# Order of VectorE's work on a stretch of attention scores: four mask additions in a row, the running maxima behind them

## The chip, the cores and the metric

The kernel runs on one core of a Trainium2 chip, in fp32 throughout. The metric is the device time of one execution in microseconds (us), as the median of several runs. Five engines work side by side, each through its own queue in order: TensorE (PE: matmuls, with weight loads shown as PEld), VectorE (DVE), ScalarE (ACT), GpSimd (POOL) and SyncE (SP, which here issues the transfers). They wait for one another through semaphores.

## The reference, cut to what matters

One block of a network over 32 batch elements of 64 tokens of width 256, with a context of 1601 keys for each element:

```python
x = x + cross_attention(layernorm(x), ctx, ctx, mask, ...)   # 16 heads of 16, 1601 keys
x = x + span_attention(layernorm(x), ...)                    # 64 keys, scores from a distance
x = x + ffn(layernorm(x), ...)                               # shared part and 8 experts
```

In the cross attention the scores are `q @ k / 4`; where the mask is false a score is set to a very low value; the softmax runs over the 1601 keys; and its weights form a sum over the values. Queries, keys and values have biases. The kernel adds a mask term (0 or -1e30) to the scores, subtracts the maximum over the keys, takes the exponential, and divides by the sum at the end.

## The kernel before, in words

**Tiling.** The unit of the cross attention is a *half*: one batch element `b` and eight of its sixteen heads (`c` is 0 or 1), so 64 halves, numbered `n`. The keys are cut into 13 blocks of 124, which stand on the partitions, and the blocks into four groups of 4, 3, 3 and 3 (`GROUPS`). One half's work on one group is a *stretch*, with `g` from 0 to 3. In a stretch, `scores` makes the scores of four pairs of heads in four banks of PSUM; VectorE adds the mask term and writes the result into SBUF (`prob`, L487, the *add*), four adds to a stretch.

**Pipeline.** Iteration `n` of the main loop (L678 on) makes the scores of half `n + 1` in its four stretches and meanwhile finishes half `n`. The maximum over the keys is formed in two steps. First VectorE keeps a running maximum over blocks in `mrun`, a bank of PSUM (`maximum`, L508): block 0 is copied there by ScalarE (`first_maxima`, L500), blocks 1 to 12 follow one by one, and the twelfth goes into `mx` in SBUF. Each reads what the one before it wrote. Then TensorE turns `mx` (`pm`, L515), VectorE reduces it along rows (`mc`, L522), TensorE spreads the result (`pb`, L530), and ScalarE copies it out (`mb`, L534). GpSimd subtracts `mb` from the four pairs of half `n` (L539, one pair in each stretch), ScalarE takes exponentials (L544), and TensorE multiplies by the values (`values`, L554): for half `n - 1`, heads 0 to 3 at the start of iteration `n`, heads 4 to 7 behind `pb` in the first stretch.

**Around it.** In every stretch TensorE also projects the keys of a following element (`pk`, L443), and in most its values (`pv`, L459). What follows the cross attention of two elements (normalisation, span attention) is cut into small steps which `run` hands out at the end of a stretch (`span_steps`, `query_steps`, `finish_steps`); many are short VectorE operations (L179 to L346, L627 to L635). The pattern of steps repeats every four iterations, since one tile of 128 tokens holds two elements of two halves each. Iterations are called R0, R1, R2 and R3 here, after `n` modulo 4.

**What sets the order.** The order on TensorE, VectorE, ScalarE and GpSimd is that of the code (`manual_schedule`). The tiles of `mm_bank` share six banks of PSUM (`ps_x`); which bank a tile gets is decided when the program is built. A matmul waits until the bank's last reader is done: VectorE for scores, ScalarE for `pk` and `pv`. Scores of the next stretch therefore wait for adds of the stretch before. The matmuls of a stretch run over blocks outside and over the four banks inside, so the first block already touches all four.

**Maxima before.** In stretches 1, 2 and 3 three blocks each have their maximum taken in `scores`, one behind each of the first three adds; these blocks come from the group before. The last three blocks follow at the end of the iteration. In stretch 0 there are only adds, with the reduction L522 behind the second.

Of the kernel before, what the change touches and what calls it, by code (L numbers as in the profile page):

```python
# [30 lines left out]
NKC = 13  # L31
KPAD = CHUNK * NKC
GROUPS = [(0, 4), (4, 3), (7, 3), (10, 3)]
BETWEEN = [(), (1, 2, 3), (4, 5, 6), (7, 8, 9), (10, 11, 12)]
LN_EPS = 1e-5
MASKED = -1e30
BIG = 3e38
# [37 lines left out]
def perceiver_kernel(ctx: ExitStack, tc: tile.TileContext, a: dict[str, bass.AP], out: bass.AP):  # L75
# [16 lines left out]
    def mm_bank(name: str):  # L92
        return ps_mm.tile([P, 512], F32, tag="mm", name=name)
# [277 lines left out]
    def pair_of(n: int, j: int):  # L371
        return prob[:CHUNK, place(n, j // 2), j % 2]

    def block_of(n: int, k: int):

        first, last = place(n, 0), place(n, 1)
        return prob[:CHUNK, first : last + 1 : last - first, :, k, :]
# [23 lines left out]
    def query_steps(t: int):  # L401
        spread = spread_of(xs[t], f"q{t}")
        yield 1
        xn = normalised(xs[t], spread, f"q{t}")
        yield 1
        ps = transposed(xn, f"q{t}")
        xnT = work.tile([P, 2, P], F32, tag="xnT", name=f"xnT_{t}")
        nc.vector.tensor_copy(xnT, ps)
        yield 1
        pq = mm_bank(f"pq_{t}")  # L410
        for c in range(2):
            for i in range(2):
                nc.tensor.matmul(
                    pq[:, c * P : (c + 1) * P], lhsT=wqT[:, i, c * P : (c + 1) * P],
                    rhs=xnT[:, i, :], start=(i == 0), stop=(i == 1),
                )

        q = work.tile([P, 2, 2, 2, S], F32, tag="qbd", name=f"qbd_{t}")
        for c in range(2):
            for e in range(2):  # L420
                nc.scalar.activation(
                    q[:, c, :, e, :], pq[:, c * P : (c + 1) * P].rearrange("p (b q) -> p b q", b=2),
                    AF.Identity, bias=bq4[:, c, e : e + 1], scale=own4[:, e : e + 1],
                )
        qbd[t] = q
        yield 1

        nc.gpsimd.tensor_tensor(xs[t], xs[t], bo_row, ALU.add)

    def load_context(b: int):  # L430
        for g in range(len(GROUPS)):
            load_piece(b, g)
        if b % 2 == 0 and b // 2 + 1 < NTILE:
            t = b // 2 + 1
            load_x(t)

    def project_keys(b: int, c: int, g: int):

        c0, n = GROUPS[g]
        k0, kn = c0 * CHUNK, min(n * CHUNK, KEYS - c0 * CHUNK)  # L440
        ps = mm_bank(f"pk_{b}_{c}_{g}")
        for i in range(2):
            nc.tensor.matmul(  # L443
                ps[:, :kn], lhsT=wkT[:, i, c * P : (c + 1) * P], rhs=cts[b][g][:, i, :kn],
                start=(i == 0), stop=(i == 1),
            )
        nc.scalar.activation(  # L447
            kTs[c][:, k0 : k0 + kn], ps[:, :kn], AF.Identity, bias=cols[:, B_K + c : B_K + c + 1]
        )
# [17 lines left out]
            ps[:kn, : n * D].rearrange("p (n h d) -> p n h d", n=n, d=DK),  # L467
        )

    def scores(n: int, g: int, between=(), then=None):  # L470

        b, c = halves[n]
        c0, nb = GROUPS[g]
        pss = [mm_bank(f"psc_{b}_{c}_{g}_{j}") for j in range(4)]
        for k in range(nb):
            for j, ps in enumerate(pss):
                at = (c0 + k) * CHUNK
                nc.tensor.matmul(  # L478
                    ps[:CHUNK, k * P : (k + 1) * P],
                    lhsT=kTs[c][32 * j : 32 * j + 32, at : at + CHUNK],  # L480
                    rhs=qbd[b // 2][32 * j : 32 * j + 32, c, b % 2, :, :],
                    start=True, stop=True, tile_position=(32 * j, 0),
                )
        between = deque(between)
        held = then() if then else None
        for j, ps in enumerate(pss):
            nc.vector.tensor_tensor(  # L487
                pair_of(n, j)[:, c0 : c0 + nb, :].rearrange("p k (e q) -> p k e q", e=2),
                ps[:CHUNK, : nb * P].rearrange("p (k e q) -> p k e q", k=nb, e=2),
                madd[:CHUNK, c0 : c0 + nb, None, :].to_broadcast([CHUNK, nb, 2, S]), ALU.add,  # L490
            )
            if between:
                maximum(n, between.popleft())
            if j == 1 and held is not None:
                maxima_of_rows(*held)

    mxs: dict[int, bass.AP] = {}

    def first_maxima(n: int):
        nc.scalar.copy(mrun[:CHUNK].rearrange("p (r i) q -> p r i q", r=2), block_of(n, 0))  # L500

    def maximum(n: int, k: int):

        dst = mrun
        if k == NKC - 1:
            dst = mxs[n] = work.tile([P, 4, P], F32, tag="mx", bufs=1, name="mx")
        dst, run = (m[:CHUNK].rearrange("p (r i) q -> p r i q", r=2) for m in (dst, mrun))
        nc.vector.tensor_tensor(dst, block_of(n, k), run, ALU.max)  # L508

    def turned_maxima(n: int):  # L510

        m = mxs.pop(n)
        ps = mm_bank("pm")
        for j in range(4):
            nc.tensor.transpose(  # L515
                ps[:, j * CHUNK : (j + 1) * CHUNK], m[:CHUNK, j, :], ident[:CHUNK, :CHUNK]
            )
        return ps, work.tile([P, 4], F32, tag="mc", name="mc")

    def maxima_of_rows(ps, col):  # L520

        nc.vector.tensor_reduce(  # L522
            col, ps[:, : 4 * CHUNK].rearrange("p (j k) -> p j k", j=4), AX.X, ALU.max
        )
# [18 lines left out]
    def exponentials(n: int, j: int):  # L543
        nc.scalar.activation(pair_of(n, j), pair_of(n, j), AF.Exp)  # L544

    def values(n: int, r: int):

        b, c = halves[n]
        v = vs[b % 2]
        for k in range(NKC):  # L550
            kn = min(CHUNK, KEYS - k * CHUNK)
            for j in range(4):
                h = 4 * r + j
                nc.tensor.matmul(  # L554
                    pvs[32 * j : 32 * j + DK + 1, c, :, r, :],
                    lhsT=v[:kn, k, 8 * c + h, :],
                    rhs=pair_of(n, h // 2)[:kn, k, (h % 2) * S : (h % 2) * S + S],
                    start=(k == 0), stop=(k == NKC - 1), tile_position=(0, 32 * j),
                )
# [95 lines left out]
        project_keys(0, 0, g)  # L655
        next(queries)
    for g in range(len(GROUPS)):
        scores(0, g, BETWEEN[g])
        if g == 0:
            first_maxima(0)  # L660
        project_keys(0, 1, g)
    for k in BETWEEN[-1]:
        maximum(0, k)

    pb = mm_bank("pbv")
# [12 lines left out]
    for n, (b, c) in enumerate(halves[:-1]):  # L678
        if c == 0 and b + 1 < B:
            load_context(b + 1)  # L680
        if c and b % 2 == 0 and b // 2 + 1 < NTILE:
            agenda[4 * n + 1].append(query_steps(b // 2 + 1))

        def project(f, *args):
            if b + 1 < B:
                f(b + 1, *args)

        if n:
            values(n - 1, 0)
            exponentials(n - 1, 3)  # L690
        for g in range(len(GROUPS)):
            if g == 0:
                turned = []

                def turn():
                    turned.extend(turned_maxima(n))
                    return turned

                scores(n + 1, g, BETWEEN[g], turn)
                project(project_keys, c, 0)  # L700
                m = maxima_along_rows(turned[1])
                if n:
                    values(n - 1, 1)
                    if c == 0:
                        agenda[4 * n + 1].append(finish_steps(b - 1, 4 * n + 1))
            else:
                scores(n + 1, g, BETWEEN[g])
                project(project_keys, c, g)
                if g == 1:
                    project(project_values, 3 * c)  # L710
                elif g == 2 and c:
                    project(project_values, 4)
                elif g == 3:
                    for u in range(5 if c else 1, 7 if c else 3):
                        project(project_values, u)
            less_maxima(n, g, m, nc.gpsimd)
            run(4 * n + g)
            for u in extra.get(4 * n + g, ()):
                linear_factor(u)
            if g == 0:  # L720
                first_maxima(n + 1)
            else:
                exponentials(n, g - 1)
        for k in BETWEEN[-1]:
            maximum(n + 1, k)


# [174 lines left out]
```

## Time and profile before

| | us |
|---|---|
| median of 3 runs | 1612.97 (1610.87 to 1616.4) |
| profiled execution, its own time | 1611.86 |
| its span, first to last instruction | 1609.8 |
| TensorE busy (matmuls) | 1548.2 |
| VectorE busy | 1260.5 |
| GpSimd busy | 1118.8 |
| ScalarE busy | 900.4 |
| adds (L487), 1024 | 582.2 |
| running maxima (L508), 704 and 64 | 483.4 and 43.9 |

"Busy" is time in which an instruction of the engine runs. Ends of matmuls are modelled, so a busy TensorE can still be waiting in part. "Idle before" a group is the engine's idle time just ahead of it, with what ended it. A timeline lists instructions in order of time with start, duration and number. A view by windows gives, for each stretch of time, the busy time of each engine, the clock granted to TensorE (1.00 is full) and the share of the DMA engines. The mean granted clock of the execution is 0.993.

### The profile page before, as it was taken

Reading aid. Unit: us, or ns where it says so; the run is one execution under the profiler, and the core shown is the slowest. Engines: PE = TensorE matmul, PEld = TensorE weight load, DVE = VectorE, ACT = ScalarE, POOL = GpSimd, SP = SyncE. Lnnn points to the kernel's source line nnn. Section 1 sums busy time; section 2 is a strip of 40 time slices with the busy share of each in tenths; the row PEclk is TensorE's granted clock in tenths of the full one; section 3 lists DMA queues with packets and bytes.
Section 4 is the critical chain, followed back from the end, with each engine's and each line's share of the span. In section 5 each row is a group of like instructions: output and inputs, shape, how many; then the busy total and the mean of one; then the engine's idle time right before and its main releaser. Section 6 shows DMA issues by size and latency. Waiting matters only on the chain.

```text
span 1609.8 us, 55500 instructions
## 1 busy us (share of the span) xinstructions
PE 1548.2 (96%) x24996; PEld 1159.3 (72%) x24996; DVE 1260.5 (78%) x2700; ACT 900.4 (56%) x1229; POOL 1118.8 (69%) x424
## 2 busy tenths in 40 slices
PE   8999999999999999999999999999999999998999
PEld 5777777777777777777777777777777777764588
DVE  4888879888887889888888879888887889886300
ACT  3555656565665656565565656565565656556411
POOL 1777768768696768768687768868687768862620
PEclk9999999999999999999999999999999999999999
DMA  5111111111110111111111111111111111104200
GB/s 170 55 31 43 34 40 34 49 44 43 49 43 28 43 40 33 50 43 43 50 43 37 36 39 34 49 44 43 49 43 32 39 37 34 34 3 130 78 24 30
DMA packets 52044, 73.32 MB, mean 46 GB/s; under 512 B 3812, under 2 KB 51040, under 8 KB 51680
## 3 DMA queue, kind: packets, MB, share of 16 engines
q1 hardware_dynamic: 50992, 69.00, 14.6%
q8 instruction: 196, 3.21, 0.8%
q10 hardware_dynamic: 816, 0.79, 0.1%
q14 instruction: 40, 0.33, 0.1%
HBM read 65.57 MB, written 4.19 MB: 43 GB/s over the span
## 4 chain that ended last, share of the span: by engine, by line
PE 59%; DVE 37%; issue 2%; ACT 1%; DMA 1%; POOL 0%; ACTq 0%; SPq 0%; DVEq 0%; POOLq 0%
DVE mrun L508 13%; DVE prob L487 13%; PE pv L459 13%; PE pk L443 13%; PE pvs L554 9%; PE psc L478 8%; PE py L832 3%; PE u L583 3%; PE pm L515 2%; PE ph L814 2%; PE pb L530 1%; DVE total L305 1%; DVE least L300 1%; DVE mrun L285 1%; PE pval L244 1%
## 5 line engine op out<-in xcount | busy, mean ns | idle before, releaser
L539 POOL TENSOR_TENSOR prob<-prob,mb 124x1664 f32<-124x1664 f32 x252 | 934.1, 3725 | 323.9 <-ACT mb L534 317.1
L487 DVE TENSOR_TENSOR prob<-psc,madd 124x384 f32<-124x384 f32 (+1 forms) x1024 | 582.2, 582 | 176.0 <-PE psc L478 175.9
L508 DVE TENSOR_TENSOR mrun<-prob,mrun 124x512 f32<-124x512 f32 x704 | 483.4, 687 | 7.0 <-ACT mrun L500 4.0
L443 PE MATMUL pk<-ct,wkT_sb 128*128 128x372 f32 (+2 forms) x1024 | 414.6, 529 | 14.8 <-DMA wkT_sb<-in_wkT 5.3
L544 ACT ACTIVATE prob<-prob 124x1664 f32<-124x1664 f32 x256 | 401.5, 1587 | 15.6 <-POOL prob L539 12.6
L459 PE MATMUL pv<-wvT_sb,ct 128*124 128x256 f32 (+1 forms) x1664 | 388.7, 382 | 0.0
L459 PEld LDWEIGHTS pv<-wvT_sb,ct 128*124 128x124 f32 (+1 forms) x1664 | 313.6, 188 | 80.4 <-DVE prob L487 3.4
L478 PE MATMUL psc<-qbd,kT 32*124 32x128 f32 x6656 | 293.9, 286 | 27.0 <-DVE prob L487 24.1
L478 PEld LDWEIGHTS psc<-qbd,kT 32*124 32x124 f32 x6656 | 230.5, 181 | 102.1 <-DVE prob L487 64.3
L447 ACT ACTIVATE kT<-pk,cols 128x372 f32<-128x372 f32 (+2 forms) x256 | 152.0, 594 | 261.8 <-PE pk L443 261.3
L443 PEld LDWEIGHTS pk<-ct,wkT_sb 128*128 128x128 f32 x1024 | 176.8, 192 | 120.6 <-issue 33.3
L465 ACT COPY v<-pv 124x512 f32<-124x512 f32 (+1 forms) x224 | 124.7, 557 | 222.2 <-PE pv L459 222.2
L554 PE MATMUL pvs<-prob,v 124*17 124x64 f32 x13312 | 212.3, 220 | 0.0
L554 PEld LDWEIGHTS pvs<-prob,v 124*17 124x17 f32 x13312 | 189.9, 98 | 26.9 <-issue 25.4
L834 DVE SCALAR_TENSOR_TENSOR ot<-py,prob 128x256 f32<-128x256 f32 x16 | 6.8, 425 | 75.7 <-PE py L832 75.7
L583 PE MATMUL u<-xfT,sw_sb 128*128 128x512 f32 x128 | 57.4, 599 | 0.4 <-DVE xfT L346 0.4
L530 PEld LDWEIGHTS pb<-cst,mc 128*124 128x124 f32 x256 | 29.6, 134 | 35.7 <-DVE mc L522 30.0
L515 PE MATMUL pm<-cst,mx 124*128 124x124 f32 x256 | 40.3, 280 | 8.7 <-DVE mx L508 7.8
L508 DVE TENSOR_TENSOR mx<-prob,mrun 124x512 f32<-124x512 f32 x64 | 43.9, 686 | 2.2
L821 ACT ACTIVATE hT<-ph,cols 128x256 f32<-128x256 f32 x32 | 13.4, 471 | 56.2 <-PE ph L814 56.2
L583 PEld LDWEIGHTS u<-xfT,sw_sb 128*128 128x128 f32 x128 | 23.6, 190 | 27.4 <-issue 24.8
L522 DVE TENSOR_REDUCE mc<-pm 128x4 f32<-128x496 f32 x64 | 42.5, 664 | 0.8 <-PE pm L515 0.8
(126 smaller groups left out, 1133.7 us busy)
## 6 DMA issues: line engine op xcount, KB each, us to landing
ct<-in_ctxT SPq DMA_DIRECT2D x64, 372.0 KB, 3.2
ct<-in_ctxT SPq DMA_DIRECT2D x32, 496.0 KB, 3.5
ct<-in_ctxT SPq DMA_DIRECT2D x32, 361.0 KB, 3.1
w<-in_w SPq DMA_DIRECT2D x16, 256.0 KB, 6.1
x<-in_x SPq DMA_DIRECT2D x16, 128.0 KB, 2.1
x_kept<-x SPq DMA_DIRECT2D x16, 128.0 KB, 1.7
prob<-x_kept SPq DMA_DIRECT2D x8, 256.0 KB, 5.5
out<-ot SPq DMA_DIRECT2D x16, 128.0 KB, 1.9
```

What stands on the lines that cost most here:

```text
L443: nc.tensor.matmul(ps[:, :kn], lhsT=wkT[:, i, c * P : (c + 1) * P], rhs=cts[b][g][:, i, :kn], start=(i == 0), stop=(i == 1),)
L447: nc.scalar.activation(kTs[c][:, k0 : k0 + kn], ps[:, :kn], AF.Identity, bias=cols[:, B_K + c : B_K + c + 1])
L459: nc.tensor.matmul(ps[:kn, n * D : (n + 1) * D], lhsT=cts[b][g][:, i, k0 : k0 + kn], rhs=wvT[:, i, :], start=(i == 0), stop=(i == 1),)
L465: nc.scalar.copy(vs[b % 2][:kn, 2 * u : 2 * u + n, :, :DK], ps[:kn, : n * D].rearrange("p (n h d) -> p n h d", n=n, d=DK),)
L478: nc.tensor.matmul(ps[:CHUNK, k * P : (k + 1) * P], lhsT=kTs[c][32 * j : 32 * j + 32, at : at + CHUNK], rhs=qbd[b // 2][32 * j : 32 * j + ...
L487: nc.vector.tensor_tensor(pair_of(n, j)[:, c0 : c0 + nb, :].rearrange("p k (e q) -> p k e q", e=2), ps[:CHUNK, : nb * P].rearrange("p (k e ...
L508: nc.vector.tensor_tensor(dst, block_of(n, k), run, ALU.max)
L515: nc.tensor.transpose(ps[:, j * CHUNK : (j + 1) * CHUNK], m[:CHUNK, j, :], ident[:CHUNK, :CHUNK])
L539: engine.tensor_tensor(sj, sj, m[:CHUNK, j, None, :].to_broadcast([CHUNK, NKC, P]), ALU.subtract)
L544: nc.scalar.activation(pair_of(n, j), pair_of(n, j), AF.Exp)
L554: nc.tensor.matmul(pvs[32 * j : 32 * j + DK + 1, c, :, r, :], lhsT=v[:kn, k, 8 * c + h, :], rhs=pair_of(n, h // 2)[:kn, k, (h % 2) * S : ( ...
L583: nc.tensor.matmul(ps, lhsT=w[:, c, hc * P : (hc + 1) * P], rhs=xfT[:, c, :, slot], start=(c == 0), stop=(c == 1),)
```

## The change

In stretches 1 to 3 the three maxima are no longer put between the adds: all four adds come first, then the three maxima, then the stretch's small operations, which stood behind the last add before. The number and form of instructions are the same on every engine. The list of blocks has a new name and the same content; the three maxima at the end of an iteration stay where they were, and so does the reduction L522 behind the second add of stretch 0.

```diff
-BETWEEN = [(), (1, 2, 3), (4, 5, 6), (7, 8, 9), (10, 11, 12)]
+BEHIND = [(), (1, 2, 3), (4, 5, 6), (7, 8, 9), (10, 11, 12)]
...
-    def scores(n: int, g: int, between=(), then=None):
+    def scores(n: int, g: int, behind=(), then=None):
...
-        between = deque(between)
         held = then() if then else None
         for j, ps in enumerate(pss):
             nc.vector.tensor_tensor(
...
             )
-            if between:
-                maximum(n, between.popleft())
             if j == 1 and held is not None:
                 maxima_of_rows(*held)
+        for k in behind:
+            maximum(n, k)
```

More of the change, by code (lines that the diff above doesn't have):

```diff
@@ L657, in perceiver_kernel @@
     for g in range(len(GROUPS)):
-        scores(0, g, BETWEEN[g])
+        scores(0, g, BEHIND[g])
         if g == 0:
@@ L661, in perceiver_kernel @@
         project_keys(0, 1, g)
-    for k in BETWEEN[-1]:
+    for k in BEHIND[-1]:
         maximum(0, k)
@@ L697, in turn @@
                     return turned
-                scores(n + 1, g, BETWEEN[g], turn)
+                scores(n + 1, g, BEHIND[g], turn)
                 project(project_keys, c, 0)
@@ L706, in perceiver_kernel @@
             else:
-                scores(n + 1, g, BETWEEN[g])
+                scores(n + 1, g, BEHIND[g])
                 project(project_keys, c, g)
@@ L723, in perceiver_kernel @@
                 exponentials(n, g - 1)
-        for k in BETWEEN[-1]:
+        for k in BEHIND[-1]:
             maximum(n + 1, k)
```

## The prediction

> **What bounds the kernel now.** I read the page first: shares, the chain that ended last, the costliest groups.
>
> ```profile
> PE 1548.2 (96%) x24996; PEld 1159.3 (72%) x24996; DVE 1260.5 (78%) x2700; ACT 900.4 (56%) x1229; POOL 1118.8 (69%) x424
> ...
> PE 59%; DVE 37%; issue 2%; ACT 1%; DMA 1%; POOL 0%; ACTq 0%; SPq 0%; DVEq 0%; POOLq 0%
> ...
> L487 DVE TENSOR_TENSOR prob<-psc,madd 124x384 f32<-124x384 f32 (+1 forms) x1024 | 582.2, 582 | 176.0 <-PE psc L478 175.9
> L508 DVE TENSOR_TENSOR mrun<-prob,mrun 124x512 f32<-124x512 f32 x704 | 483.4, 687 | 7.0 <-ACT mrun L500 4.0
> ```
>
> TensorE is not simply full: the chain runs over VectorE for 37%, mostly adds and maxima. They take turns, so I ask which sets the end in which iteration. The view by windows, cut at the starts of `pm` for one repetition of R2, R3, R0, R1 (89.83 us; 14 such make up most of the span):
>
> ```profile
> 799.24:822.14 22.90, 21.48 (x368) 15.94 (x368) 21.85 (x55) 12.71 (x19) 19.35 (x8) 1.00 0.01 4
> 822.14:843.70 21.56, 21.28 (x373) 16.14 (x373) 17.37 (x31) 13.86 (x18) 18.32 (x6) 1.00 0.28 78
> 843.70:867.20 23.50, 22.47 (x407) 16.99 (x403) 20.05 (x45) 12.63 (x18) 15.89 (x6) 1.00 0.04 14
> 867.20:889.07 21.87, 21.87 (x388) 16.85 (x389) 17.72 (x36) 14.70 (x22) 15.29 (x5) 1.00 0.27 77
> ```
>
> The fourth figure is VectorE's. In R2 it is busy 21.85 of 22.90 us; R3 and R1 leave it 4 us free, R0 3.5. So VectorE is the bound in R2, TensorE in R3 and R1. For R0 I read TensorE's timeline where the scores of stretch 3 begin:
>
> ```profile
> 856.48 0.48 PE L478 MATMUL psc<-qbd,kT 32*124 32x128 f32 x2
> 857.20 0.48 PE L478 MATMUL psc<-qbd,kT 32*124 32x128 f32 x4 [0.24 <-DVE prob L487]
> 858.26 0.91 PE L478 MATMUL psc<-qbd,kT 32*124 32x128 f32 x18 [0.58 <-DVE prob L487]
> 859.32 1.48 PE L443 MATMUL pk<-ct,wkT_sb 128*128 128x361 f32 x4
> ```
>
> The four banks come free one by one as stretch 2's adds are done: 2.84 us from the first matmul to `pk`, where a free run needs 0.86 (826.40 to 827.27). That is 1.98 us lost. From such starts the losses are 2.95 us in R2 (0.94, 0.10, 1.54, 0.37), 0.82 in R3, 2.12 in R0 and 0.07 in R1: 5.96 a repetition.
>
> Last, the clock. Six of the fourteen R0 (first at 209.86) last 25.17 to 25.20 us, the others 23.50. The view by windows inside a long one:
>
> ```profile
> 1037.84:1041.25 3.41, 2.45 (x27) 1.74 (x27) 3.38 (x8) 2.15 (x3) 3.40 (x1) 1.00 0.14 38
> 1041.25:1044.66 3.41, 3.41 (x8) 2.31 (x7) 3.34 (x10) 0.56 (x1) 2.75 (x2) 0.50 0.00 0
> ```
>
> TensorE waits for banks in the first, and the next 3.41 us are granted half the clock. Each costs 25.19 - 23.50 = 1.69 us; six cost 10.1.
>
> [...] a maximum right behind a maximum, which reads what that one wrote, starts later than one behind an add (below). [...] Here 3.41 us at 0.50 follow a window that was only partly idle.
>
> **The change part by part.** *The DVE block of a stretch.* Start to start, add to next is 0.468 us, an independent maximum to the next add 0.595: 4 x 0.468 + 3 x 0.595 = 3.66 (827.35 to 831.01). The maxima at an iteration's end show the price of a row:
>
> ```profile
> 819.95 1.42 DVE L508 TENSOR_TENSOR mrun<-prob,mrun 124x512 f32<-124x512 f32 x2
> 821.40 0.69 DVE L508 TENSOR_TENSOR mx<-prob,mrun 124x512 f32<-124x512 f32 x1
> 822.01 1.28 DVE L487 TENSOR_TENSOR prob<-psc,madd 124x512 f32<-124x512 f32 x2
> ```
>
> 0.72 to the second (820.67), 0.73 to the third, 0.61 to what follows. After: 1.87 + 0.72 + 0.73 + 0.61 = 3.93, so +0.27 a stretch, +0.81 an iteration. Bounds: 0 if all overlapped, +0.4 if the first maximum waited too. *Release.* The fourth add ends 3 x 0.468 + 0.55 = 1.95 us after the first one starts, instead of 3 x 1.063 + 0.55 = 3.74; the fourth bank comes 1.8 us earlier. *What moves back:* the small operations, by 0.27 us, and with them GpSimd's and ScalarE's steps behind them. No transfer moves.
>
> R3: stretch 2's third add ends at 832.69 + 0.94 + 0.55 = 834.18, before TensorE asks at 834.48; the 0.82 goes. `pm` can start at 842.88. VectorE: 827.35 + 3.93 + 1.42 (L305, L306) + 3.93 + 4.05 (three more maxima follow) + 2.14 = 842.82. Both fit: **-0.82**.
>
> R0: starts 0.82 earlier. VectorE is then without a gap from the add at 848.53 to `mx`: before 17.70, less 0.34 (the wait for `tr_f`, now covered), plus 0.81, gives 866.70; `pm` 866.75 instead of 867.20. TensorE waits some 1.5 us there, so its regained 1.98 brings nothing: **+0.37**.
>
> R1: TensorE's bound; the +0.81 lies in VectorE's idle gaps (0.56, 0.29, 0.49): **-0.07**.
>
> R2: from the add at 806.27 to the end of `mx` VectorE had only one gap, 0.24 for ScalarE's copy L500, which the adds now cover: +0.81 - 0.24 = **+0.57**. TensorE's 2.95 us are idle elsewhere. GpSimd's subtractions are 1.2 us ahead of the values' need, and R2 gets no shorter, so they stay hidden.
>
> Sum: -0.82 + 0.37 - 0.07 + 0.57 = +0.05 a repetition, +0.7 over 14. In the first iterations `pm` moves up by TensorE's lost time until `mx`, later by 0.27 a stretch, holds it. In n = 0, `pm` at 59.63 could come 0.71 earlier, but `mx` ends at 59.28: -0.3. Likewise n = 1, 2 and 4 give -0.1, -0.5 and +0.4, and the last iteration, where nothing is lost to banks, +0.6: +0.1.
>
> *The clock.* In R0 the scores of stretch 3 wait about 0.8 us instead of 1.98, so I expect no half clock there: **-10.1**. In R2 TensorE now reaches stretch 3's scores at 810.81, and the third add is done only at 806.27 + 3.93 + 1.29 + 1.49 = 812.98: 2.2 us lost in one place, so half clock may come there; six of fourteen R0 had it, with the slightly longer wait I take 7 of 14. It costs less: behind it lie 7.54 us of work until `pm` (1.33 + 3.55 + 1.58 + 1.08), to 821.41, and `mx` is done at 822.66: 1.25 us are spare, 0.44 remain. 7 x 0.44 = **+3**. If the bank waited for is the fourth add's, 0.47 later, it is +6.
>
> All: 0.7 + 0.1 - 10.1 + 3 = -6.3 against the profiled 1611.86, which stands 1.1 below the median: about **1607 us** beside 1612.97.
>
> **The rivals.** *The half clock moves at full price.* R2's windows are hit as often as R0's were, and the spare 1.25 us is not there: 7 x 1.69 - 10.1 + 0.8 = +2.5, **1615**; within 0.3%. For it: the same length of wait. Against it: `pm` must wait for `mx` anyway.
>
> *Slower: half clock on the closing chain.* In R0 and R2 TensorE now waits 1.3 to 1.5 us just ahead of `pm`. Should that bring half clock, it falls on `pm`, `pk`, `pb`, values and scores, 5.3 us with VectorE idle behind (2.29 us at 827.35), and nothing covers it. 40% of 28 places x 1.69 = 19, less 10.1: **1622**. It decides from seven such places on. Against it: the window holds 1.08 us of scores, `pm` and values, more than R0's 2.45 us window did.
>
> *Much faster: TensorE is the true bound.* All 5.96 us come back: 14 x 5.96 + 10 = 93, **1520**; half of it 1566. For it: 96% busy. Against it: R2's 21.85 of 22.90 us on VectorE. I give it little.
>
> **How the numbers follow.** The main case (1600 to 1612) has 0.50, the half clock moved 0.25, slower 0.17, much faster 0.08. 0.3% (4.8 us) is about what this measurement can tell from no change, so faster means below 1608.1. The main case gives 0.30 faster and 0.20 same, the second 0.05, 0.19 and 0.01, which makes faster 0.43, same 0.39, slower 0.18. Low 1595: maxima in a row at +0.2 in place of +0.27 (six stretches of R0 and R2, 14 times: -5.9), no half clock in R2 (-3), and 3 for the spread of the runs. High 1622 is the slower case. The likeliest case alone is 1600 to 1612.
>
> **What would show it.** Repetitions of 89.8 us, R3 shorter by 0.8, R2 longer by 0.6; maxima 0.72 us apart; TensorE waiting for `mx` (L508) ahead of `pm` in R0 and R2 rather than for adds; no R0 of 25.2 us, some half clock in R2. Wrong, if R2 gets shorter (VectorE wasn't its bound), or if half clock follows the wait at `pm`.

## The result and the profile after

Over 20 runs each the median is 1610.11 us after the change and 1612.43 before; the ratio is 0.9982 with a 95% interval of 0.9975 to 0.9989. The change gains 2.3 us, clear of noise and below the 0.3% (4.8 us) that the prediction set as the least that it would call faster. The runs also lie closer together: 1608.47 to 1611.69 after, 1609.30 to 1617.14 before.

The page of the kernel after the change, in the order shown of before (shares, the chain that ended last, the adds and the maxima; L487 and L508 are now L486 and L507):

```profile
PE 1547.5 (96%) x24996; PEld 1157.6 (72%) x24996; DVE 1294.8 (81%) x2700; ACT 901.6 (56%) x1229; POOL 1119.6 (70%) x424
...
PE 59%; DVE 37%; issue 2%; ACT 0%; DMA 0%; POOL 0%; DVEq 0%; ACTq 0%; POOLq 0%
...
L486 DVE TENSOR_TENSOR prob<-psc,madd 124x384 f32<-124x384 f32 (+1 forms) x1024 | 536.6, 581 | 148.8 <-PE psc L478 147.7
L507 DVE TENSOR_TENSOR mrun<-prob,mrun 124x512 f32<-124x512 f32 x704 | 487.2, 692 | 16.1
```

The chain's shares are unchanged. VectorE is busy 34 us longer with the same 2700 instructions. A maximum lasts hardly longer (692 for 687 ns), but the second and third of a row no longer begin while the operation ahead of them is still running: they start 0.72 and 0.73 us behind it. An add lasts as long as before (581 for 582 ns); the group's busy time falls from 582.2 to 536.6 us because the ends of adds now overlap each other rather than a maximum.

The view by windows for one repetition (R2, R3, R0, R1 from the starts of `pm`), to be held against 22.90, 21.56, 23.50 and 21.87 before; the fourth figure is VectorE's:

```profile
706.22:729.67 23.45, 21.51 (x369) 15.99 (x369) 22.43 (x55) 13.38 (x19) 19.90 (x8) 1.00 0.02 5
729.67:750.51 20.84, 20.84 (x372) 15.96 (x373) 17.87 (x31) 13.31 (x18) 17.78 (x6) 1.00 0.29 80
750.51:774.38 23.87, 23.02 (x407) 17.18 (x403) 20.69 (x46) 13.37 (x19) 15.91 (x6) 1.00 0.05 14
774.38:796.30 21.92, 21.92 (x388) 16.85 (x389) 18.08 (x36) 13.97 (x21) 15.28 (x5) 1.00 0.27 74
```

R2 is 0.55 us longer, R0 0.37 longer, R3 0.72 shorter, R1 0.05 longer: 90.08 against 89.83 us, a repetition that is 0.25 us longer. VectorE's timeline in R2 shows the new blocks:

```profile
713.25 1.94 DVE L486 TENSOR_TENSOR prob<-psc,madd 124x384 f32<-124x384 f32 x4
715.11 2.15 DVE L507 TENSOR_TENSOR mrun<-prob,mrun 124x512 f32<-124x512 f32 x3
717.16 0.46 DVE L626 STREAM_TRANSPOSE pvs<-pvs 128x256 f32<-128x256 f32 x1
```

Four adds from 713.25 to the first maximum at 715.11, three maxima to 717.16: 3.91 us where the alternating order takes 3.66 when nothing holds it. At this very place it took 3.99 before, from 806.27 to 810.26, because the first maximum waited for ScalarE's copy:

```profile
806.27 0.55 DVE L487 TENSOR_TENSOR prob<-psc,madd 124x384 f32<-124x384 f32 x1
807.06 0.70 DVE L508 TENSOR_TENSOR mrun<-prob,mrun 124x512 f32<-124x512 f32 x1 [0.24 <-ACT mrun L500]
...
810.26 0.45 DVE L627 STREAM_TRANSPOSE pvs<-pvs 128x256 f32<-128x256 f32 x1
```

So in R2 this stretch gains a little, and stretches 2 and 3 pay. And TensorE's timeline in the same R2, at the scores of stretch 3 and at `pm`:

```profile
717.89 0.48 PE L478 MATMUL psc<-qbd,kT 32*124 32x128 f32 x2
719.03 1.84 PE L478 MATMUL psc<-qbd,kT 32*124 32x128 f32 x22 [0.66 <-DVE prob L486]
...
727.25 1.15 PE L478 MATMUL psc<-qbd,kT 32*124 32x128 f32 x32
729.67 0.61 PE L514 MATMUL pm<-cst,mx 124*128 124x124 f32 x4 [1.28 <-DVE mx L507]
```

TensorE gets there earlier and waits, first for the adds and then 1.28 us for `mx`. What it won by early banks it hands back at `pm`.

The clock is the other half of the result. In the profiled execution no R0 of the main loop has half clock any more; four R2 have it (n = 6, 26, 34, 54). The view by windows inside one, n = 34:

```profile
808.11:811.52 3.41, 2.73 (x26) 1.93 (x27) 3.34 (x8) 2.91 (x3) 3.41 (x3) 1.00 0.00 0
811.52:814.93 3.41, 3.41 (x8) 2.32 (x7) 3.38 (x7) 0.73 (x2) 3.41 (x2) 0.50 0.00 0
```

Such an R2 lasts 23.80 instead of 23.46 us, so half clock costs 0.34 there; in R0 it cost 1.69 before.

### The profile page after: what moved, and what is told of

The parts are those of the page before. It is cut to its first block, busy times and chain, and to the rows that moved or that the text cites. A ratio compares the mean times of both kernels' runs of the same rounds, so it can differ in the third digit from the quotient of the medians.

```text
span 1606.5 us, 55516 instructions
## 1 busy us (share of the span) xinstructions
PE 1547.5 (96%) x24996; PEld 1157.6 (72%) x24996; DVE 1294.8 (81%) x2700; ACT 901.6 (56%) x1229; POOL 1119.6 (70%) x424
## 4 chain that ended last, share of the span: by engine, by line
PE 59%; DVE 37%; issue 2%; ACT 0%; DMA 0%; POOL 0%; DVEq 0%; ACTq 0%; POOLq 0%
PE pk L443 14%; DVE mrun L507 13%; PE pv L459 13%; DVE prob L486 12%; PE psc L478 9%; PE pvs L553 8%; PE py L831 3%; PE u L582 3%; PE pm L514 2%; PE ph L813 2%; PE pb L529 1%; DVE mx L507 1%; DVE mrun L285 1%; PE pval L244 1%; PE psa L315 1%
## 5 line engine op out<-in xcount | busy, mean ns | idle before, releaser
L486 DVE TENSOR_TENSOR prob<-psc,madd 124x384 f32<-124x384 f32 (+1 forms) x1024 | 536.6, 581 | 148.8 <-PE psc L478 147.7
L507 DVE TENSOR_TENSOR mrun<-prob,mrun 124x512 f32<-124x512 f32 x704 | 487.2, 692 | 16.1
L514 PEld LDWEIGHTS pm<-cst,mx 124*128 124x128 f32 x256 | 26.3, 140 | 38.8 <-issue 22.0
L507 DVE TENSOR_TENSOR mx<-prob,mrun 124x512 f32<-124x512 f32 x64 | 43.9, 686 | 2.2
```

Source lines behind the costliest of these rows:

```text
L486: nc.vector.tensor_tensor(pair_of(n, j)[:, c0 : c0 + nb, :].rearrange("p k (e q) -> p k e q", e=2), ps[:CHUNK, : nb * P].rearrange("p (k e ...
L514: nc.tensor.transpose(ps[:, j * CHUNK : (j + 1) * CHUNK], m[:CHUNK, j, :], ident[:CHUNK, :CHUNK])
```

## The experiments

The theory: VectorE bounds R2 and R0, and a row of maxima, each held by the one before it, makes them longer by what R3 gains; the net gain is R0's half clock. The main rival: R2 and R0 are longer because small operations and everything behind them moved back behind the maxima, whatever these cost each other. All experiments choose, by half and stretch, the add behind which each of the three maxima stands: (0, 1, 2) is the kernel before, (3, 3, 3) the one after. In the profiles of the experiments the same code stands at other lines, and the diffs show only what differs, with comments added. Here `n` in the code is the half whose scores are made, one more than the iteration's number.

### The row without its dependences: norow and norow2

```diff
         if k == NKC - 1:
             dst = mxs[n] = work.tile([P, 4, P], F32, tag="mx", bufs=1, name="mx")
+        elif k < 10 and k % 3:
+            dst = unread
```

and in norow2, which has two such tiles (both kernels leave two of every three blocks out of the running maximum):

```diff
-            dst = unread
+            dst = unread[k % 3 - 1]
```

> The changed order, but the first and second of the three maxima in a row write into a tile that nobody reads, so that the next one doesn't read what the last one wrote. This leaves out two of every three blocks from the running maximum. Theory (in R2 and R0 VectorE is the bound, and a maximum that reads the one before it costs 0.12 us more): the distance of the maxima falls from 0.72 to about 0.60 us, R2 from 23.46 to 22.7, R0 from 23.87 to 23.1, R3 stays near 20.8, R1 near 21.9; a repetition about 88.5 instead of 90.09, the time 1587 to 1592. Rival (R2 and R0 got longer because the small operations and all that hangs on them stand behind the maxima, whatever the maxima cost each other): R2 and R0 stay, 1610.

> As norow, but the first and the second of the three maxima write into two different tiles that nobody reads (norow had one for both, and the second was still held 0.71 us behind the first). Two of every three blocks are left out of the running maximum. Theory (a maximum is held by any operation of its own engine that it shares a tile with; each row costs 0.12 us on VectorE's path in R2 and R0): both distances 0.60 us, R2 about 22.65 (norow 23.02, after 23.46), R0 about 23.1 (23.44, 23.87), R3 and R1 as in norow; 14 x 0.7 = 10 below norow's fast part, about 1583 to 1588. Rival (only the read matters, and what is left of R2's length is the later small operations): R2 23.0, R0 23.4, 1592.

Measured: norow 1592.81 us (ratio to before 0.9888, 0.9872 to 0.9905), norow2 1585.61 (0.9842, 0.9827 to 0.9857). In norow R2 was 23.02, not 22.7, and R0 23.44, because only one of the two distances fell: from the first maximum to the second it was 0.709 us, from the second to the third 0.605. The first two shared an output tile; the third shares with the second only what both read, and was not held. The instruction records of the traces say more: every maximum that starts 0.71 to 0.73 us behind another (128 in the kernel before, 532 in the one after) waits for a semaphore that VectorE itself raises, and of the freed ones in norow and norow2, 0.595 to 0.605 behind, 561 of 576 have no such wait. So what a row costs is this wait for the operation just ahead, as the program is built. VectorE's timeline of norow2, with two tiles:

```profile
706.07 1.91 DVE L492 TENSOR_TENSOR prob<-psc,madd 124x384 f32<-124x384 f32 x4
707.91 1.27 DVE L517 TENSOR_TENSOR unread<-prob,mrun 124x512 f32<-124x512 f32 x2
709.10 0.69 DVE L517 TENSOR_TENSOR mrun<-prob,mrun 124x512 f32<-124x512 f32 x1
709.70 1.94 DVE L492 TENSOR_TENSOR prob<-psc,madd 124x384 f32<-124x384 f32 x4
```

From 707.91 to 709.70 three maxima take 1.79 us, as much as three alternating ones (3 x 0.595). The view by windows of norow2 for R2 and R0:

```profile
694.11:716.76 22.65, 21.51 (x369) 15.98 (x369) 21.85 (x55) 12.68 (x18) 19.11 (x7) 1.00 0.02 7
...
737.46:760.53 23.07, 22.55 (x407) 17.03 (x403) 20.10 (x46) 13.17 (x19) 15.90 (x6) 1.00 0.04 14
```

R2 falls step by step with the rows: 23.46, 23.02, 22.65; R0 likewise 23.87, 23.44, 23.07. Apart from the output tiles, the operations and the place of the small ones are those of the kernel after. So the rival, as an explanation of the longer R2 and R0, is out. With the row's waits gone the new order is 1.6% faster than the kernel before, though norow2 doesn't compute the whole maximum.

### One iteration's part alone: r3_only and r0r2_only

```diff
-    return (3, 3, 3)
+    return (3, 3, 3) if n % 4 == 0 and n else (0, 1, 2)   # r3_only
+    return (3, 3, 3) if n % 2 else (0, 1, 2)              # r0r2_only
```

> The new order in R3's stretches alone, the old one elsewhere. Theory (R3 is TensorE's, and gains its lost 0.8 us; R0 keeps its waits for banks and so its half clock): R3 20.85, R0 23.50 with about six of 25.2, R2 22.90, R1 21.88; 14 x -0.7 = -10, about 1602. Rival (the only gain of the change is the half clock that left R0): no gain clear of noise, 1610 to 1613.

> The new order in all stretches of R0 and R2, the old one in R1 and R3. Theory (there VectorE is the bound, the row lengthens both, and half clock moves from R0 to R2, where it costs less): R2 23.46, R0 23.87, R3 21.55, R1 21.9; 14 x 0.93 = +13 and -10 for R0's half clock, +1 to 3 for R2's: 1614 to 1617 beside 1611. Rival (the parts do not add up, because R0's length hangs on R3's gain): R0 near 23.5, 1608 to 1611.

Measured: r3_only 1596.28 us (0.9912, 0.9897 to 0.9927), r0r2_only 1618.26 (1.0037, 1.0024 to 1.0049). The view by windows of r3_only:

```profile
704.22:727.11 22.89, 21.48 (x368) 15.94 (x369) 21.84 (x55) 12.71 (x19) 19.35 (x8) 1.00 0.02 5
727.11:747.98 20.87, 20.87 (x373) 15.98 (x373) 17.95 (x31) 13.84 (x18) 18.30 (x6) 1.00 0.29 81
747.98:771.47 23.49, 22.47 (x406) 16.98 (x403) 20.04 (x45) 12.62 (x18) 15.87 (x6) 1.00 0.05 14
```

R3 takes its gain, R2 and R0 stay as before. Three R0 of 25.19 us remained in its profile, where six were expected. Their number seems to depend on where the iterations fall: the starts of half clock lie whole multiples of 3.413 us apart (225.47 and 317.63 before: 27 of them; 180.05 and 630.61 after: 132), and in r3_only the three are 358.4 us apart, 105 of them and close to four repetitions. In r0r2_only R2 is 23.45, R0 23.86 and R3 21.52, so the lengths of the iterations add up. The times, -14.5 and +5.4 us by the medians, do not add up to -2.3, mainly because R0's half clock is gone in r0r2_only and, by luck, half gone in r3_only (3 x 1.69 = 5.1 us, counted twice); R3's own gain is 14 x 0.69 = 9.6 us. The R0 and R2 half of the change is a loss of 0.4%, a little above the 1614 to 1617 us expected, although R0's half clock is gone; three R2 have it instead.

### The wait that brings half clock: r0_stretch2

```diff
-    return (3, 3, 3)
+    return (3, 3, 3) if n % 4 == 1 and g == 2 else (0, 1, 2)
```

> The new order in stretch 2 of R0 alone, whose adds the scores of stretch 3 wait for. Theory (the half clock follows that wait): no R0 of 25.2 us; R0 about 23.4 (0.27 us for the row, against the 0.34 us in which VectorE waited for a transposition); all else as before; -10, about 1602. Rival (the half clock comes from elsewhere in the iteration or at random): it stays in 4 to 7 of 14, 1611 to 1613.

Measured: 1599.56 us (0.9928, 0.9912 to 0.9944). All fourteen R0 last 23.33 or 23.34 us, none has half clock, and the other iterations are those of before (22.90, 21.55, 21.88). TensorE's timeline where the scores of R0's stretch 3 begin:

```profile
760.11 1.96 PE L484 MATMUL psc<-qbd,kT 32*124 32x128 f32 x24
762.00 1.18 PE L449 MATMUL pk<-ct,wkT_sb 128*128 128x361 f32 x3
```

From the first matmul to `pk` it takes 1.89 us instead of 2.84, so the wait fell from 1.98 to 1.03 us. One stretch in sixteen, with no other wait shortened, takes all of R0's half clock away. So it hung on this wait, and the place of the windows alone doesn't bring it.

### Maxima one add later: shift and mix

```diff
-    return (3, 3, 3)
+    return (1, 2, 3)                                      # shift
+    return (0, 1, 2) if n % 4 == 3 else (1, 2, 3)         # mix: R2 as before
```

> The three maxima each one add later than before: add, add, maximum, add, maximum, add, maximum. No two maxima in a row inside a stretch, and the adds end 0.6 us earlier than before. Theory: R2 22.7 (ScalarE's copy is covered, no row), R3 20.85, R0 23.1, R1 21.9: 88.5 a repetition, -19; the half clock leaves R0 (-10) and may cost up to 7 in R2: about 1590, below both kernels. Rival (small operations behind the maxima make R0 and R2 longer; the row is not the price): R2 23.2 or more, R0 23.5 or more, 1605 or more.

> The order of before in R2, that of shift (a maximum behind the second, third and fourth add) elsewhere. Theory (shift's half clock in R2 comes because TensorE, let go earlier in stretch 1, waits in one piece in stretch 3; the old order splits that wait): R2 22.90 and no half clock there, R3 20.92, R0 23.07, R1 21.88: 88.8 a repetition, 1585 to 1588, steadier from run to run than shift. Rival (half clock in R2 is a matter of the window grid and comes with the shorter repetition): some R2 of 24 to 25.7 us, 1592 or more.

Measured: shift 1594.70 us, with runs from 1586.88 to 1604.49 (ratio 0.9899, 0.9868 to 0.9930); mix 1587.21 (1586.65 to 1588.53; 0.9846, 0.9832 to 0.9860). Shift's iterations are as expected, R2 22.65, R3 20.92, R0 23.07, R1 21.88, but six of its fourteen R2 from n = 6 on had half clock and lasted 24.08 to 25.74, so it came to 1595 instead of 1590: one window of half clock made 24.08, two in a row made 25.74. TensorE's timeline at the scores of R2's stretches 2 and 3, first shift:

```profile
714.35 0.93 PE L484 MATMUL psc<-qbd,kT 32*124 32x128 f32 x24
715.22 1.52 PE L449 MATMUL pk<-ct,wkT_sb 128*128 128x372 f32 x4
716.66 0.48 PE L484 MATMUL psc<-qbd,kT 32*124 32x128 f32 x2
717.54 0.94 PE L484 MATMUL psc<-qbd,kT 32*124 32x128 f32 x4 [0.40 <-DVE prob L492]
719.07 1.18 PE L484 MATMUL psc<-qbd,kT 32*124 32x128 f32 x18 [0.58 <-DVE prob L492]
```

and mix, the same place:

```profile
707.11 0.49 PE L484 MATMUL psc<-qbd,kT 32*124 32x128 f32 x6
707.85 0.92 PE L484 MATMUL psc<-qbd,kT 32*124 32x128 f32 x18 [0.24 <-DVE prob L492]
710.35 0.76 PE L484 MATMUL psc<-qbd,kT 32*124 32x128 f32 x4
711.70 0.92 PE L484 MATMUL psc<-qbd,kT 32*124 32x128 f32 x20 [0.58 <-DVE prob L492]
```

In shift stretch 2's scores run through at 714.35 and all the waiting falls on stretch 3, from 716.66 to 719.07. In mix it is split in two, with `pk` between them. In all, shift loses less: in an R2 at full clock (n = 34) 2.4 us in stretch 3, where mix loses 0.9 in stretch 2 and 1.5 in stretch 3. The view by windows of shift around that place:

```profile
716.17:719.58 3.41, 2.43 (x24) 1.37 (x23) 3.34 (x9) 2.68 (x4) 3.41 (x3) 1.00 0.00 0
719.58:722.99 3.41, 3.41 (x15) 2.11 (x10) 3.41 (x8) 0.79 (x1) 3.41 (x2) 0.50 0.00 0
```

The profile of mix has no half clock in any iteration of the main loop. The nine traces fit this: where R2's wait lies in one piece (after, norow, norow2, r0r2_only, shift), 4, 1, 5, 3 and 6 of fourteen R2 have half clock; where it is split (before, r3_only, r0_stretch2, mix), none of 56. No run splits the wait and changes nothing else, so that the split is the cause stays an inference. Mix computes all that the kernel before does, and beats both kernels: it is 1.5% faster than the one before by the ratio above, and 1.4% faster than the one after by the medians (1587.21 against 1610.11 us, from different runs).

## Why the prediction was right, step by step

Range and main case held: 1610.11 lies in 1595 to 1622 and in 1600 to 1612, and a small gain came. The main case is wide enough to hold no gain at all, though, and the point was too high: 1607 against 1612.97, a gain of 6.0, where 2.3 were measured; the likeliest class by the stated chances, faster at 0.43, did not come. The steps against the profiled executions, for fourteen repetitions (n = 6 to 61), in us:

| step | predicted | measured |
|---|---|---|
| R3 gains the wait for banks | 14 x -0.82 = -11.5 | -9.9 |
| R0 longer, VectorE its bound | 14 x 0.37 = +5.2 | 14 x 0.37 = +5.2 |
| R0 loses half clock | -10.1 | -10.1 |
| R0, other | 0 | +1.5 |
| R1 | 14 x -0.07 = -1.0 | +0.7 |
| R2 longer, VectorE its bound | 14 x 0.57 = +8.0 | 14 x 0.56 = +7.8 |
| R2 gets half clock | 7 x 0.44 = +3 | 4 x 0.34 = +1.4 |
| first and last iterations | +0.1 | +0.2 |
| span | -6.3 | -3.3 |

**The mechanism held**, and the two steps in which VectorE is the bound came to 0.01 us an iteration. The price of a row could be read before the change from the three maxima at the end of an iteration (0.72, 0.73), and norow2 shows that it is what lengthens R2 and R0: without it R2 is 0.80 us shorter than after, by the working 0.81. That the two sums came so close is in part luck. A covered gap was worth more than its idle time, because an operation that nothing holds starts 0.08 us before the one ahead of it ends: 0.33 us for the 0.24 in R2, 0.42 for the 0.34 in R0. Against that, `pm` begins 0.15 us behind the end of `mx` in both after the change, where the working had 0.05. The two errors, some 0.1 us each, cancel. The 96% of TensorE were no evidence of its being the bound: the "much faster" rival fell with R2.

**Half clock.** That it would leave R0, and come to R2 at a lower price, was right. R2's reserve ahead of `mx` was 1.25 us by the working; the measured 0.34 means 1.69 - 0.34 = 1.35, and the trace agrees: `pm` comes 2.43 us behind the start of the last scores, where R3 shows 1.08 without a wait. In norow, whose R2 waits 1.06 us there, half clock cost 0.63, again 1.69 in sum. In shift, whose R2 is 0.8 us shorter, it cost 1.43 (24.08 - 22.65) where it lasted one window. The slower rival, half clock after the wait at `pm`, did not come in the kernel after. One size was wrong here without harm. The working had R0's scores of stretch 3 wait 0.8 us; they wait 1.30 (2.16 to `pk`, less the free 0.86), and so the wait at `pm` is 0.79 us and not 1.5:

```profile
763.29 2.23 PE L478 MATMUL psc<-qbd,kT 32*124 32x128 f32 x24
765.45 1.48 PE L443 MATMUL pk<-ct,wkT_sb 128*128 128x361 f32 x4
```

Half clock left R0 all the same.

**Sizes that were off.** The working had R3 freed of all 0.82 us and R1 of 0.07. In the profile after, the scores of R3's stretch 3 still take 1.00 us to the next matmul instead of 0.86, and in R1 those of stretch 2 take 0.92. These are waits of 0.05 to 0.14 us. The profile puts R3's down to the adds, and R1's to ScalarE's copy of `pval` (L250), for which this `pk` did not wait before; which bank a matmul waits for depends on the assignment when the program is built, which the prediction could not see. R1's 0.07 was no bank wait at all: its last scores take 1.15 us before and after (1.08 in R3), and each time `pm` starts 0.15 us behind the end of `mx`, as it does in R0 and R2, where it plainly waits for `mx`. R3 and R1 together are 3.3 us worse than the working. That this is about the 3.0 by which the sum was short is again a cancellation: R2's half clock cost 1.6 us less than expected, and R0 lost 1.5 to something else. This is two late R0 (n = 56 and 60), which lasted 24.24 and 25.04 us instead of 23.87. TensorE's timeline of the kernel after, in the scores of stretch 1 of n = 56:

```profile
1296.50 0.91 PE L478 MATMUL psc<-qbd,kT 32*124 32x128 f32 x19
1297.89 0.49 PE L478 MATMUL psc<-qbd,kT 32*124 32x128 f32 x5 [0.47 <-issue]
```

TensorE stops there with nothing that the profile shows it waiting for. Two to four R0 from n = 48 on are longer in norow, norow2, shift and r0r2_only too, which all change R2, and none in the kernel before, r3_only, r0_stretch2 and mix, which leave it. What it is stays open; no run here tests it.

## What to carry to other kernels

Before reordering an engine's queue, ask in each stage which engine has no gaps: here earlier release of banks gained where VectorE, which releases them, was not itself the bound (R3 0.72 us shorter) and not where it was (R2 0.55 and R0 0.37 us longer). The same edit can so gain in one stage and lose in another (r3_only -0.9%, of which about 0.3% is half clock that it missed by luck, and r0r2_only +0.4%). Look for the price of the new neighbourhood in the trace: maxima that wait for the one just ahead of them on VectorE, because they share a tile with it, cost 0.72 to 0.73 us each in a row and 0.595 spread among adds. And where the granted clock falls to 0.50 behind waits, as here, look at where waits gather, since splitting one may be worth more than shortening it: mix waits longer than shift in R2, in two pieces, and is 0.5% faster by the medians.

## What the runs showed of the hardware that was not expected

- A write behind a write to the same tile cost VectorE nearly as much as a read behind a write: 0.709 us from start to start in norow against 0.595 with separate tiles in norow2, and 0.72 to 0.73 where the second reads what the first wrote. In both cases the program makes the second wait for a semaphore that VectorE raises. Whether the engine would hold it without that wait, no run shows.
- An operation of VectorE that nothing holds starts before the one ahead has ended: adds of 0.548 us follow each other at 0.465 in the kernel after. A gap in the trace therefore costs some 0.08 us more than the idle time that it shows.
- Half clock came after windows of 3.41 us in which TensorE was busy 2.43 us (shift) to 3.01 us (norow2) by the profile, so well before it stood idle. In the main loop it lasted one window each time, except in three of shift's six R2, where it lasted two. Busy time alone does not decide it. This window of the kernel after, across R2's wait at `pm`, has less than any of those, and full clock followed:

```profile
726.22:729.63 3.41, 2.18 (x112) 1.88 (x100) 3.34 (x6) 2.29 (x3) 3.41 (x2) 1.00 0.02 5
```

- A sum over matmuls that counts their rows sorts the windows better. As an estimate, take 0.89 ns for each column of a matmul (eight `pv` matmuls of 256 columns take 1.82 us in mix from the first start, 705.29, to the next group, 707.11), multiply by its rows as a share of 128, the most that a matmul here has (one of scores has 32, one of `values` 124), spread this over the matmul's record, and add it up in each window of 3.41 us. From 90 to 1412 us of the nine traces 29 windows at full clock were followed by half clock, and they come to 1.00 to 1.33 us; the 3414 others come to 1.35 us or more. Without the weight by rows the two overlap. The bound is not exact: with each matmul's work put at one end of its record, windows between 1.28 and 1.42 us go either way. The sum was found after the runs, and none was made to test it; that the rows matter to the clock is not shown.
